# Counting the edges of an adjacency matrix by fours in a two-layer graph network

## The chip, the cores and the metric

The kernel runs on one core of a Trainium2 chip. The metric is the device time of one execution in microseconds. Inputs and outputs lie in the chip's main memory (DRAM), and the time covers the whole program from the first load to the last store. Engines are named as in the profile: PE does matrix products, PEld is its weight load, DVE, ACT and POOL are the vector, scalar and general engine, and SP issues transfers.

## What is computed

`x` is 4096 x 512 float32, `adj` is 4096 x 4096 int32 of zeros and ones with a density of 0.0078 (some 32 edges a row). Two layers follow each other, each with a residual and a layer norm:

```python
Ab = A > 0
keep = Ab & (jnp.cumsum(Ab.astype(jnp.int32), axis=1) <= 64)
cnt = keep.sum(axis=1, keepdims=True)
nb_mean = (keep.astype(X.dtype) @ X) / jnp.maximum(cnt, 1.0)
xj = leaky_relu(nb_mean @ W_nb.T + b_nb)
xi = leaky_relu(X @ W_line.T + b_line)
layer0 = xi + jnp.where(cnt > 0, xj, 0)
# layer 1, with h the normed result of layer 0 plus x:
Wh = h @ W + bW
e = leaky_relu((Wh @ a1 + b1)[:, None] + (Wh @ a2 + b2)[None, :], 0.2)
e = jnp.where(adj > 0, e, -9e15)
layer1 = softmax(e, axis=1) @ Wh
```

What matters here is `keep`: of each row of `adj` only the first 64 edges count in layer 0, while layer 1 uses every edge. So each edge needs a mark that says "kept", "edge but not kept" or "no edge".

## The kernel before

The rows are cut into 32 blocks of 128, one row to a partition, and a block of `adj` into two chunks of 2048 columns: 64 chunks, counted by `s`. Each chunk goes through a small pipeline:

1. `load_adj` (L156, queue of SP) loads 128 x 2048 int32, 1 MB.
2. `edge` (L163, ACT) makes ones and zeros in bf16 with a steep sigmoid (L167), and sums them along the row into `cnts`.
3. `scan` (L172, DVE) runs along the row: a value starts at 66 and each column takes `max(value, 2) - edge` (L179). After the k-th edge it is 66 - k, so 65 down to 2 for the 64 kept edges, and 1 for every later one. The last value is carried to the row's second chunk through `ends` (L183). Multiplied by the edge itself (L184) this is the code: 0 for no edge, 1 for an edge that is not kept, 2 and more for one that is. Every second block, `count` (L189) turns `ends` into the number of kept edges.
4. `pack` (L198, ACT) casts the code to one byte (L202), and POOL's queue stores it in `code_d` (L203).

Layer 0's neighbour sum reads the codes of a block back with a transposing transfer (L428, L460), and `make_kt` (L248, ACT, L254) turns them into the 0/1 weights of the matmuls at L521 with a sigmoid whose threshold, `steep[:, 1:2]`, lies between 1 and 2. Layer 1 reads the codes again (L616) and masks by whether they are zero (L635).

The order on every engine is the order in which the program issues, written out by hand (`manual_schedule`). There are three stages around the change. In the first (span 36 to 235 us) row block `i` is multiplied by both weights of layer 0 (`linear`, L342, matmuls at L345). DVE transposes the x blocks for it (`turn_x`, L293, L299) and does additions (L375, L383, L435), ACT evicts PSUM (L413) and bends lines (L379). `codes_until` (L207) puts 20 chunks evenly among these rows: per step one load, `edge(q + 1)`, `scan(q)`, `pack(q - 1)`. In the second (235 to 700 us) PE does `keep @ (X W)`: 32 rows of blocks in four steps of 16 matmuls (L521), the tiles `kt` made two steps ahead in one of three buffers. `codes_step` (L235) adds 25/16 chunks to each row until all 64 are done, some 660 us into the span; here `scan` is issued at once, while `edge` and `pack` wait in `late_q` and come out one or two at a time behind a `make_kt` (`codes_late`, L229). The third stage is layer 1 and has no chunks. The tiles `a`, `edge`, `left` and `code` have two buffers each; the x blocks turned for the matmuls have three, and the PSUM accumulators six.

The lines that set this order in the second stage:

```python
        make_kt(s + 2)
        if g == 2:
            bend0(i - 1)
        codes_late()
...
        codes_step(start + int((s + 1) * RATE / NS))
```

Of the kernel before, what the change touches and what calls it, by code (L numbers as in the profile page):

```python
# [11 lines left out]
BF16 = mybir.dt.bfloat16  # L12
U8 = mybir.dt.uint8
I32 = mybir.dt.int32
AF = mybir.ActivationFunctionType
ALU = mybir.AluOpType
# [4 lines left out]
P = 128  # L21
SQ = 32
NEIGHBORS = 64.0
# [3 lines left out]
FAR = 1e30  # L27

STEEP = 4000.0
# [3 lines left out]
def two_layer_adj_gnn(  # L33
# [16 lines left out]
    nc = tc.nc  # L50
    N, C = x.shape
    NB = N // P
    NC = C // P
    NT = NB // 2
    CH = 2048
    NCH = N // CH
# [17 lines left out]
    ps_acc = ctx.enter_context(tc.tile_pool(name="ps_acc", bufs=6, space=PSUM))  # L74

    few = const.tile([P, 5], F32, name="few")
    two, steep, far, neg_half = few[:, 0:1], few[:, 1:3], few[:, 3:4], few[:, 4:5]
    for k, value in enumerate((2.0, -0.5 * STEEP, -1.5 * STEEP, FAR, -0.5)):
        nc.vector.memset(few[:, k : k + 1], value)


# [4 lines left out]
    ends = const.tile([P, NB], F32, name="ends")  # L86
# [50 lines left out]
    with ExitStack() as l0:  # L137
        adj_p = l0.enter_context(tc.tile_pool(name="l0_adj", bufs=2))
# [13 lines left out]
        loaded = {}  # L152
        edge_of = {}
        seen_of = {}

        def load_adj(s):  # L156
            if s < NB * NCH:
# [2 lines left out]
                nc.sync.dma_start(a, adj_blk(b)[:, ts(h, CH)])  # L160
                loaded[s] = a

        def edge(s):  # L163
            if s < NB * NCH:
                b, h = divmod(s, NCH)
                edge_of[s] = adj_p.tile([P, CH], BF16, name="edge")
                nc.scalar.activation(  # L167
                    edge_of[s], loaded.pop(s), AF.Sigmoid, bias=steep[:, 0:1], scale=STEEP,
                    accum_out=cnts[:, h, b : b + 1],
                )  # L170

        def scan(s):  # L172
            if s < NB * NCH:
                b, h = divmod(s, NCH)

                left = adj_p.tile([P, CH], BF16, name="left")
                e = edge_of.pop(s)
                end = ends[:, b : b + 1]
                nc.vector.tensor_tensor_scan(  # L179
                    left, two.to_broadcast([P, CH]), e,  # L180
                    NEIGHBORS + 2.0 if h == 0 else end, ALU.max, ALU.subtract,
                )
                nc.vector.tensor_copy(end, left[:, CH - 1 : CH])  # L183
                nc.vector.tensor_tensor(left, e, left, ALU.mult)  # L184
                seen_of[s] = left
                if h == NCH - 1 and b % 2:
                    count(b - 1)

        def count(b):  # L189
            two_b = slice(b, b + 2)  # L190
            cnt = stat.tile([P, 2], F32, name="cnt")
            nc.vector.tensor_scalar(cnt, ends[:, two_b], 2.0, -1.0, ALU.max, ALU.mult)
            nc.vector.tensor_scalar_add(cnt, cnt, NEIGHBORS + 2.0)
            nc.vector.tensor_scalar(some[:, two_b], cnt, 0.0, None, ALU.is_gt)
            nc.vector.tensor_scalar_max(cnt, cnt, 1.0)
            nc.vector.reciprocal(rcnt[:, two_b], cnt)

        def pack(s):  # L198
            if 0 <= s < NB * NCH:
                b, h = divmod(s, NCH)  # L200
                code = adj_p.tile([P, CH // 2], BF16, name="code")
                nc.scalar.copy(code.bitcast(U8), seen_of.pop(s))  # L202
                nc.gpsimd.dma_start(code_d[b][:, ts(h, CH // 2)], code)  # L203

        done = [0]
# [1 line left out]
        def codes_until(s):  # L207

            while done[0] < min(s, NB * NCH + 1):
                q = done[0]  # L210
                if q == 0:
                    load_adj(0)
                    load_adj(1)
                    edge(0)
                load_adj(q + 2)
                edge(q + 1)
                scan(q)
                pack(q - 1)
                done[0] += 1
# [5 lines left out]
        def pack_late(q):  # L225
            pack(q)
            packed[0] = q + 1
# [7 lines left out]
        def codes_step(s):  # L235
            while done[0] < min(s, NB * NCH + 1):
                codes_late(2)
                q = done[0]
                load_adj(q + 2)
                scan(q)  # L240
                late_q.extend([(edge, q + 1), (pack_late, q - 1)])
                done[0] += 1
# [17 lines left out]
        with ExitStack() as la:  # L260
# [44 lines left out]
            def early(name):  # L305
                dt = I32 if name == "a" else BF16
                t = adj_p.tile([P, CH], dt, name=name).bitcast(F32)
                return t.rearrange("p (c q) -> p c q", q=C)

            raw = {}  # L310
            for name in ("nb", "line"):
                t = early("a")
                raw[name] = [t[:, c, :] for c in range(NC)]
            raw["w"] = []
            for k in range(2):
                t = early("left")
                raw["w"] += [t[:, c, :] for c in range(NC // 2)]
            early_rows = []
            for k in range(2):
                t = early("edge")  # L320
# [482 lines left out]
    cnt, idle = cnts[:, 0, :], cnts[:, 1, :]  # L803
# [17 lines left out]
    for s in range(NS):  # L821
# [13 lines left out]
        if FIRST <= s < FIRST + 8:  # L835
            b, i = divmod(s - FIRST, NI)
            mask(b, i)
            score(b, i)
        if FIRST + 4 <= s < FIRST + 12:
            b, i = divmod(s - FIRST - 4, NI)  # L840
# [4 lines left out]
        if s in range(FIRST + 14, FIRST + 22, 2):  # L845
            q, part = divmod((s - FIRST - 14) // 2, 2)
# [5 lines left out]
    for q in range(NP * NT):  # L852
        g, k = divmod(q, NP)
# [5 lines left out]
        b = {2: 2 * g + 3, 3: 2 * g + 4}.get(k, 2 if q == 0 else NB)  # L859
# [29 lines left out]
    p, rz = banks[NT - 1], rzs[NT - 1]  # L889
# [59 lines left out]
```

## Time and profile before

| | us |
|---|---|
| median of 3 runs | 1599.97 (1599.85 to 1600.56) |
| the profiled execution | 1600.12 |
| its span, first instruction to last | 1598.4 |
| PE busy in it | 1579.6 |
| DVE busy | 1305.4 |
| ACT busy | 924.2 |
| scans, L179, 64 of them | 284.5 |
| products, L184, 64 | 78.4 |
| edges, L167, 64 | 127.4 |
| packs, L202, 64 | 120.5 |

The busy row of the page gives, for each engine, the busy time in us, its share of the span and (x) the number of instructions. The chain of waits goes back from the last instruction, at each step to what released it, and gives each engine's share of the span. A wait reads "who waited, its line <- for whom: us in total, times, longest". A group or tile row gives the line, engine and operation, the count, the duration in ns (mean, or minimum/median/maximum) and the shape as partitions x elements with types, the output first. Busy matmuls are modelled and overlap, so the time from the start of one to the start of the next tells PE's pace better than the busy share. The granted clock of PE is 0.997 of full speed over the span.

### The profile page before, as it was taken

How to read it: one execution, taken by the hardware profiler on the slowest of the kernel's cores; microseconds unless marked ns; L12 is line 12 of the kernel's file. 1: busy time of each engine (PE TensorE's matmuls, PEld its weight loads, DVE VectorE, ACT ScalarE, POOL GpSimd, SP SyncE). 2: the span in 40 equal slices, each digit the busy share in tenths (PEclk: the TensorE clock that was granted, in tenths of full speed). 3: DMA queues.
4: the chain of work that ended last, by engine and by line, in shares of the span. 5: the costliest groups of instructions: out<-in, count | busy, mean ns of one | idle time of the engine just before them, and what ended most of it. 6: DMA issues, size and time to landing. Idle time of an engine off the chain costs nothing.

```text
span 1598.4 us, 18483 instructions
## 1 busy us (share of the span) xinstructions
PE 1579.6 (99%) x6456; PEld 1218.4 (76%) x6456; DVE 1305.4 (82%) x2154; ACT 924.2 (58%) x1086; POOL 260.0 (16%) x396
## 2 busy tenths in 40 slices
PE   8999999999999999999999999999999999999997
PEld 4444448888888888864378888888888888888886
DVE  4999986999999999555888887878888888788863
ACT  2655556777777777514237755557755557655520
POOL 4455531122223122210000000000000000000000
PEclk9999999999999999999999999999999999999999
DMA  8887867676757666444201111111111111211100
GB/s 195 287 259 236 265 217 224 215 220 211 229 189 228 206 215 191 116 103 122 76 27 28 53 54 41 52 36 34 53 47 47 48 28 44 54 41 53 40 7 33
DMA packets 168364, 192.73 MB, mean 121 GB/s; under 512 B 101408, under 2 KB 134464, under 8 KB 160080
## 3 DMA queue, kind: packets, MB, share of 16 engines
q1 hardware_dynamic: 147968, 131.38, 29.4%
q0 software_dynamic: 19728, 59.27, 11.0%
q8 instruction: 50, 0.82, 0.2%
q10 hardware_dynamic: 576, 0.92, 0.2%
q14 instruction: 42, 0.34, 0.1%
HBM read 132.65 MB, written 42.08 MB: 109 GB/s over the span
## 4 chain that ended last, share of the span: by engine, by line
PE 92%; DVE 3%; DMA 2%; issue 1%; ACT 1%; SPq 0%; POOL 0%; DVEq 0%; POOLq 0%; ACTq 0%
PE acc L739 34%; PE acc L521 29%; PE pt L739 14%; PE acc L345 9%; PE acc L825 5%; DMA c<-in_x_dram 1%; DVE left L179 1%; DMA a<-in_L_gnn_W_line_dram 1%; DMA edge<-in_L_gnn_a_dram 0%; DVE edge L361 0%; DVE xt L299 0%; DMA w<-x_d 0%; DVE y_lo L435 0%; DVE t L375 0%; ACT w L635 0%
## 5 line engine op out<-in xcount | busy, mean ns | idle before, releaser
L521 PE MATMUL acc<-y_hi,kt 128*128 128x512 f32 x1016 | 395.2, 389 | 0.0
L521 PE MATMUL acc<-y_lo,kt 128*128 128x512 f32 x1016 | 395.2, 389 | 0.0
L739 PE MATMUL acc<-bt,s 128*128 128x256 f32 x1536 | 342.6, 379 | 0.0
L739 PEld LDWEIGHTS acc<-bt,s 128*128 128x128 f32 x1536 | 291.8, 190 | 39.7
L635 ACT ACTIVATE w<-nat,few 128x1024 f32<-128x1024 uint8 x128 | 136.9, 1135 | 290.1 <-DVE a L699 238.8
L126 POOL TENSOR_TENSOR rs<-ve,few 128x1 f32<-128x1 f32 x64 | 76.2, 1191 | 969.3 <-DVE ve L124 969.2
L739 PE MATMUL acc<-bt,a 128*128 128x256 f32 x1024 | 232.1, 379 | 0.0
L739 PE MATMUL pt<-bt,a 128*128 128x256 f32 x1024 | 231.5, 379 | 0.0
L521 PEld LDWEIGHTS acc<-y_hi,kt 128*128 128x128 f32 x1016 | 190.8, 188 | 39.7
L521 PEld LDWEIGHTS acc<-y_lo,kt 128*128 128x128 f32 x1016 | 190.6, 188 | 39.5
L739 PEld LDWEIGHTS pt<-bt,a 128*128 128x128 f32 x1024 | 194.6, 190 | 26.9 <-issue 0.5
L254 ACT ACTIVATE kt<-ktb,few 128x1024 fp32r<-128x1024 uint8 x124 | 142.9, 1152 | 124.7 <-PE acc L521 107.8
L739 PEld LDWEIGHTS acc<-bt,a 128*128 128x128 f32 x1024 | 194.6, 190 | 26.5
L699 DVE STREAM_TRANSPOSE a<-w 128x1024 f32<-128x1024 f32 x128 | 153.0, 1224 | 57.8 <-ACT w L680 53.2
L627 ACT ACTIVATE w<-w,st_n 128x1024 f32<-128x1024 f32 x128 | 149.4, 1233 | 39.5 <-DVE m L638 39.5
L638 DVE CUSTOM_DVE_ANT_0 w<-e_n,w 128x1024 f32<-128x1024 f32 x128 | 149.6, 1221 | 9.6 <-ACT w L635 8.2
L167 ACT ACTIVATE edge<-a,few 128x2048 bf16<-128x2048 int32 x64 | 127.4, 1991 | 43.4 <-DVE left L184 20.3
L680 ACT ACTIVATE w<-w,nm 128x1024 f32<-128x1024 f32 x128 | 145.4, 1136 | 11.3 <-DVE nm L671 11.3
L179 DVE TENSOR_TENSOR_SCAN left<-few,edge 128x2048 bf16<-128x2048 f32 x32 | 141.3, 4415 | 12.7 <-ACT edge L167 10.9
L179 DVE TENSOR_TENSOR_SCAN left<-few,ends,edge 128x2048 bf16<-128x2048 f32 x32 | 143.2, 4475 | 2.3 <-ACT code L202 2.3
L202 ACT CAST code<-left 128x2048 uint8<-128x2048 bf16 x64 | 120.5, 1882 | 0.0
L345 PE MATMUL acc<-wt_nb,xt 128*128 128x512 f32 x256 | 115.5, 594 | 2.8 <-DVE xt L299 2.0
(135 smaller groups left out, 1521.3 us busy)
## 6 DMA issues: line engine op xcount, KB each, us to landing
a<-in_adj_dram SPq DMA_DIRECT2D x64, 1024.0 KB, 5.3
code_d<-code POOLq DMA_DIRECT2D x64, 256.0 KB, 3.7
nat<-code_d SPq DMA_DIRECT2D x256, 64.0 KB, 2.0
own_d<-xb POOLq DMA_DIRECT2D x32, 256.0 KB, 5.9
w<-x_d SPq DMA_DIRECT2D x128, 64.0 KB, 2.0
c<-in_x_dram POOLq DMA_DIRECT2D x124, 64.0 KB, 5.6
xb<-in_x_dram POOLq DMA_DIRECT2D x31, 256.0 KB, 5.8
own<-own_d SPq DMA_DIRECT2D x31, 256.0 KB, 2.8
```

The source lines that it names most:

```text
L167: nc.scalar.activation(edge_of[s], loaded.pop(s), AF.Sigmoid, bias=steep[:, 0:1], scale=STEEP, accum_out=cnts[:, h, b : b + 1],)
L179: nc.vector.tensor_tensor_scan(left, two.to_broadcast([P, CH]), e, NEIGHBORS + 2.0 if h == 0 else end, ALU.max, ALU.subtract,)
L202: nc.scalar.copy(code.bitcast(U8), seen_of.pop(s))
L254: nc.scalar.activation(kts[s], bytes_.rearrange("p t (i r) -> p t r i", r=2), AF.Sigmoid, bias=steep[:, 1:2], scale=STEEP,)
L345: nc.tensor.matmul(pl, lhs_t[:, k, :], w_t[name][:, k, :], start=(k == 0), stop=(k == NC - 1),)
L521: nc.tensor.matmul(accs[i], kt[:, k // 2, k % 2, :], term[:, j, :], start=(j == 0 and term is y_hi), stop=(j == NB - 1 and term is y_lo),)
L627: nc.scalar.activation(dst, src, AF.Prelu, bias=bias, scale=scale, alpha=0.2)
L635: nc.scalar.activation(w_i, nats[b, i // 2].bitcast(U8)[:, i % 2, :], AF.Relu, bias=far, scale=-FAR)
L638: nc.vector.tensor_tensor_reduce(w_i, e2_n, w_i, 1.0, -3e38, ALU.subtract, ALU.max, m4s[b][:, i : i + 1])
L680: nc.scalar.activation(w_i, w_i, AF.Exp, bias=nms[b][:, i : i + 1], accum_out=z4s[g][:, r, i : i + 1])
L699: nc.vector.transpose(a[:, r].rearrange("p s (i a) -> p i s a", a=SQ), wts[2 * g + r][:, :, ts(k, 8 * SQ)].rearrange("p i (s x) -> p i s x ...
L739: nc.tensor.matmul(banks[g][n], lhs[:, j, :], bt[:, 4 * k + j, rhs, :], start=(k == 0 and j == 0 and n == mate[0]), stop=(k == NP - 1 and ...
```

## The change

A chunk's columns are seen in groups of four neighbours. ACT's edge activation now reads the int32 columns so that `edge` holds four runs of 512: all first members of the groups, then all second, third and fourth ones. DVE adds first and second as well as third and fourth members (one instruction on 2 x 512), then the two sums (512), and scans the sums of four: 512 steps instead of 2048. The value starts at 69, is held at 5 or more, and gives what is left behind each group's fourth column. What is left behind the third is that plus the fourth's edge, behind the second the value behind the fourth plus the sum of third and fourth, and so on: one addition on 512 and one on 2 x 512. The product with the edges is as before. A kept edge now has a code of 5 or more, one that isn't kept 1 to 4, so the threshold of the weights is 4.5, and `count` uses 5 and 69. The pack reads the four runs in turn, so that the stored codes stand in the order of the columns as before. `scan` is split into two functions that are called one after the other.

```diff
--- before.py
+++ after.py
@@ -74,8 +74,8 @@
     ps_acc = ctx.enter_context(tc.tile_pool(name="ps_acc", bufs=6, space=PSUM))
 
     few = const.tile([P, 5], F32, name="few")
-    two, steep, far, neg_half = few[:, 0:1], few[:, 1:3], few[:, 3:4], few[:, 4:5]
-    for k, value in enumerate((2.0, -0.5 * STEEP, -1.5 * STEEP, FAR, -0.5)):
+    five, steep, far, neg_half = few[:, 0:1], few[:, 1:3], few[:, 3:4], few[:, 4:5]
+    for k, value in enumerate((5.0, -0.5 * STEEP, -4.5 * STEEP, FAR, -0.5)):
         nc.vector.memset(few[:, k : k + 1], value)
 
 
@@ -160,37 +160,57 @@
                 nc.sync.dma_start(a, adj_blk(b)[:, ts(h, CH)])
                 loaded[s] = a
 
+        def fours(t):
+
+            return t.rearrange("p (q t) -> p q t", q=4)
+
         def edge(s):
             if s < NB * NCH:
                 b, h = divmod(s, NCH)
-                edge_of[s] = adj_p.tile([P, CH], BF16, name="edge")
+                edge_of[s] = fours(adj_p.tile([P, CH], BF16, name="edge"))
                 nc.scalar.activation(
-                    edge_of[s], loaded.pop(s), AF.Sigmoid, bias=steep[:, 0:1], scale=STEEP,
+                    edge_of[s], loaded.pop(s).rearrange("p (t q) -> p q t", q=4),
+                    AF.Sigmoid, bias=steep[:, 0:1], scale=STEEP,
                     accum_out=cnts[:, h, b : b + 1],
                 )
 
         def scan(s):
+            scan_sums(s)
+            scan_codes(s)
+
+        def scan_sums(s):
             if s < NB * NCH:
                 b, h = divmod(s, NCH)
 
-                left = adj_p.tile([P, CH], BF16, name="left")
-                e = edge_of.pop(s)
+
+                left = fours(adj_p.tile([P, CH], BF16, name="left"))
+                e = edge_of[s]
                 end = ends[:, b : b + 1]
+                nc.vector.tensor_tensor(left[:, 0:2], e[:, 0:4:2], e[:, 1:4:2], ALU.add)
+                nc.vector.tensor_tensor(left[:, 2], left[:, 0], left[:, 1], ALU.add)
                 nc.vector.tensor_tensor_scan(
-                    left, two.to_broadcast([P, CH]), e,
-                    NEIGHBORS + 2.0 if h == 0 else end, ALU.max, ALU.subtract,
+                    left[:, 3], five.to_broadcast([P, CH // 4]), left[:, 2],
+                    NEIGHBORS + 5.0 if h == 0 else end, ALU.max, ALU.subtract,
                 )
-                nc.vector.tensor_copy(end, left[:, CH - 1 : CH])
+                nc.vector.tensor_copy(end, left[:, 3, CH // 4 - 1 :])
+                seen_of[s] = left
+
+        def scan_codes(s):
+            if s < NB * NCH:
+                b, h = divmod(s, NCH)
+                left, e = seen_of[s], edge_of.pop(s)
+
+                nc.vector.tensor_tensor(left[:, 1], left[:, 3], left[:, 1], ALU.add)
+                nc.vector.tensor_tensor(left[:, 0:4:2], left[:, 1:4:2], e[:, 1:4:2], ALU.add)
                 nc.vector.tensor_tensor(left, e, left, ALU.mult)
-                seen_of[s] = left
                 if h == NCH - 1 and b % 2:
                     count(b - 1)
 
         def count(b):
             two_b = slice(b, b + 2)
             cnt = stat.tile([P, 2], F32, name="cnt")
-            nc.vector.tensor_scalar(cnt, ends[:, two_b], 2.0, -1.0, ALU.max, ALU.mult)
-            nc.vector.tensor_scalar_add(cnt, cnt, NEIGHBORS + 2.0)
+            nc.vector.tensor_scalar(cnt, ends[:, two_b], 5.0, -1.0, ALU.max, ALU.mult)
+            nc.vector.tensor_scalar_add(cnt, cnt, NEIGHBORS + 5.0)
             nc.vector.tensor_scalar(some[:, two_b], cnt, 0.0, None, ALU.is_gt)
             nc.vector.tensor_scalar_max(cnt, cnt, 1.0)
             nc.vector.reciprocal(rcnt[:, two_b], cnt)
@@ -199,7 +219,10 @@
             if 0 <= s < NB * NCH:
                 b, h = divmod(s, NCH)
                 code = adj_p.tile([P, CH // 2], BF16, name="code")
-                nc.scalar.copy(code.bitcast(U8), seen_of.pop(s))
+                nc.scalar.copy(
+                    code.bitcast(U8).rearrange("p (t q) -> p t q", q=4),
+                    seen_of.pop(s).rearrange("p q t -> p t q"),
+                )
                 nc.gpsimd.dma_start(code_d[b][:, ts(h, CH // 2)], code)
 
         done = [0]
```

## The prediction

> **What bounds the kernel now.** I read the page first, its busy row and its chain of waits, then the busy time by stretches, cut where PE's work changes (x is the number of instructions).
>
> ```profile
> PE 1579.6 (99%) x6456; PEld 1218.4 (76%) x6456; DVE 1305.4 (82%) x2154; ACT 924.2 (58%) x1086; POOL 260.0 (16%) x396
> PE 92%; DVE 3%; DMA 2%; issue 1%; ACT 1%; SPq 0%; POOL 0%; DVEq 0%; POOLq 0%; ACTq 0%
> ```
> ```profile
> core 0: us, PE busy (x) PEld busy (x) DVE busy (x) ACT busy (x) POOL busy (x), PEclk, DMA share, GB/s
> 36.00:90.00 54.00, 51.85 (x120) 22.36 (x119) 48.29 (x49) 30.66 (x34) 23.76 (x43) 1.00 0.85 275
> 90.00:235.00 145.00, 145.00 (x339) 64.22 (x338) 139.34 (x152) 78.68 (x88) 74.45 (x135) 1.00 0.80 250
> 235.00:660.00 425.00, 425.00 (x1875) 351.57 (x1874) 383.32 (x471) 316.70 (x278) 98.33 (x103) 1.00 0.67 206
> ```
>
> PE is the bound in all three stretches in which adjacency chunks are worked: 15 of the 64 chunks in 90 to 235 us, about 44 in 235 to 660 us (43 edges, 45 packs by the groups of that window), the other five in 36 to 90 us. A pipelined engine can look busy without being at its rate, so I checked the pace in the timeline: from 450 us on the L521 matmuls start 0.2267 us apart without one exception, 64 of them to a row of blocks, so 14.5 us a row. Nothing that DVE or ACT does better can shorten that. The waits say the same from the other side: ACT waits for PE, not PE for ACT.
>
> ```profile
> ACT kt L254 <- PE acc L521: 107.8, 91, 2.5
> PEld acc L345 <- DVE xt L299: 5.1, 5, 1.9
> PE acc L345 <- DVE xt L299: 2.0, 2, 1.1
> ```
>
> The third line is all that the scan costs PE today: two gaps (0.94 us before 48.4 us and 1.10 us before 56.6 us in PE's timeline) in which PE wants a transposed x block that DVE makes only after a scan. So the most that this change can give back is 2.0 us, 0.13% of the time. Everything else DVE saves is saved beside a busy PE. What matters is whether something new gets slower than PE; the candidate is ACT, whose cover is the idle time in the third stretch: 425.0 - 316.7 = 108.3 us.
>
> **DVE, per chunk.** The rows, from the tile and shape views:
>
> ```profile
> L183 DVE CAST ends<-left x64: 153/154/157, 45.7 to 651.2; 128x1 f32<-128x1 bf16 x64
> L184 DVE TENSOR_TENSOR left<-edge,left x64: 1224/1224/1228, 45.9 to 651.4; 128x2048 bf16<-128x2048 bf16 x64
> L179 DVE TENSOR_TENSOR_SCAN left<-few,edge x32: 4409/4415/4425, 41.2 to 638.3; 128x2048 bf16<-128x2048 f32 x32
> L179 DVE TENSOR_TENSOR_SCAN left<-few,ends,edge x32: 4469/4476/4484, 49.4 to 646.7; 128x2048 bf16<-128x2048 f32 x32
> ```
>
> Two f32 tensor_tensor shapes give the fixed part: 692 ns at 512 elements (L715) and 420 ns at 256 (L768) make 1.06 ns per element and 148 ns fixed. With 148 ns fixed, the bf16 L184 runs at (1224-148)/2048 = 0.525 ns and the scan at (4415-148)/2048 = 2.08 ns per element. Now: 4.445 (mean scan) + 0.154 + 1.224 = 5.82 us. After: two additions of 1024 at 0.686, two of 512 at 0.417, the scan of 512 at 1.245 (mean of the forms), the copy 0.154, the product 1.224: together 4.83 us. DVE gains 0.99 us per chunk, 64 us in all, of which PE can use 2. All operands of the additions are runs of 512 adjacent bf16, so I take L184's pace. From the other side: if the split views made the additions run at the f32 pace, they cost 1.24 and 0.69, and a chunk takes 6.48 us, 0.66 more than now; if the product did too, 1.76 more. The new constants and the counting (L192, L193) keep their instructions. No instruction is moved in the order of any queue; no DMA is added, and the loads on SP and the stores on POOL (L203) keep place and size.
>
> **ACT, per chunk.** The instructions stay two, but both get strided reads. The edge activation (L167, median 1.987 us, int32) reads every fourth element, 16 bytes apart; the pack (L202, 1.882 us) reads its four neighbours from four runs 1024 bytes apart, a hop at every element. The trace has no such read. Bounds by rows: below, no cost: L254 already reads uint8 at a step of two (1152 ns) against 1136 ns for the same operation from its other buffer, and L635's plain read of the same size takes 1135 ns. That step stays within a few bytes, so the row is near in form and far in distance. Above: the slowest stream in the trace is the scan, 4415/2048 = 2.16 ns per element, 4.42 us for 2048: +2.43 for the edge and +2.54 for the pack. Between: the paces that this trace shows on DVE lie a factor of two apart (0.525, 1.06, 2.08 ns), and I take one such step for a read that no longer brings neighbours together. ACT's slope is (1987-1152)/1024 = 0.815 ns (L167 against L254), so a step costs 2048 x 0.815 = 1.67 us per instruction, 3.34 us per chunk. This is an estimate, near the middle of the bounds.
>
> The third stretch then needs 316.7 + (43+45) x 1.67 = 463.7 us of ACT in 425 us: 38.7 us too much. ACT works ahead by two kt tiles (make_kt(s+2); 2 x 3.63 us of matmuls less the 1.15 us of a kt, and a wait of about 0.5): 5.6 us of lag are free. PE therefore ends this stretch 33 us later. Behind the slower edge and pack in ACT's queue stand the kt activations (L254) that PE waits for; that is the new wait, PE for kt. In 90 to 235 us ACT goes to 78.7 + 15 x 3.34 = 128.8 of 145 us, which still fits; there PSUM evictions (L413) queue behind 7.2 us of edge and pack, which three rows of accumulators, 20 us of matmuls, cover. The first two PE gaps: the first scan waits for its edge (DVE's 10.9 us idle on L167), which comes 1.67 us later and gives 0.99 back; I book the gaps at zero.
>
> [...]
>
> Sum: the profiled execution took 1600.12 us (span 1598.4 and 1.7 around it), 0.15 above the median of 1599.97, so one base serves. 1600 + 33 = **1633 us**.
>
> **Rivals.**
> 1. *The strided reads are hidden (not slower).* One mechanism: ACT's idle time in the third stretch. It decides at (108.3 + 5.6)/44 = 2.59 us added per chunk; below, PE never waits for a kt. For it: L254's step of two costs at most 17 ns against L635's plain read, and if only one of the two instructions pays a step, 1.67 is below the bound. Time: 1600; with both free also the two gaps go, 1598. Against: both reads leave the neighbourhood that L254's step keeps.
> 2. *Both pay more, up to the scan's pace.* 43 x 2.43 + 45 x 2.54 = 219 us in the third stretch, less 108.3 and 5.6: +105. In 90 to 235 us 78.7 + 15 x 4.97 = 153.3, +8; before it five chunks add 25 to an idle of 23.3, +2. Time 1715. [...]
> 3. *The additions run at the f32 pace, the reads are free.* DVE in 90 to 235 us: 139.3 + 15 x 0.66 = 149.2 of 145, +4; in the third stretch 383.3 + 29 = 412 of 425, hidden. Time 1605; with the product at 1.76 more, 1600 + 21 + 36 + 6 = 1663. Against it: operands in runs like L184's.
> 4. *The change does not do what it says*: the short scan keeps a long fixed time. With 1 us more per scan DVE is where it was, and the time is decided by ACT as above.
>
> **How the numbers follow.** The forecast (both reads about one step of two) 0.46; rival 2, clearly more than that, 0.20; rival 1 0.28; rival 3 with 4's ill case 0.06. The measurement can tell about 0.2% from no change, 3.2 us. Since only 2.0 us can be won, faster by that much gets 0.02, for something on PE's path that I overlook; same 0.26, slower 0.72. The cases of no change and of a loss lie far apart, so the range goes from 1598 (rival 1) to 1720 (rival 2 and a little); the likeliest case's own range is 1608 to 1660, 2.8 to 4.0 us added per chunk with ACT's surplus landing on PE.
>
> **What would show it.** Right: scan rows of about 1.2 us, additions of 0.69 and 0.42; edge and pack rows near 3.7 and 3.6 us; in the third stretch ACT near 99% busy, DVE lower, PE with gaps, the wait "ACT kt for PE" gone and "PE for ACT kt" in its place, and the third stretch longer by some 33 us while 830 us and after are only shifted. Wrong: edge and pack at their old durations (then 1598 to 1600 and the 48 and 56 us gaps gone), or one of them alone doubled (then no change). If both rows are doubled and the time still stands, my step from ACT's surplus to PE's wait is what failed.

## The result and the profile after

The changed kernel takes **1660.27 us** (median of four, 1658.5 to 1661.05) against 1600.18 us before: a ratio of 1.0374 with a 95% interval of 1.0356 to 1.0392. The forecast was slower at 1633 us, with a range of 1598 to 1720. The profiled execution took 1661.05 us with a span of 1659.3 us, 60.9 us longer than the span before.

The busy row of the page, to be held against the same row of before:

```profile
PE 1595.0 (96%) x6456; PEld 1214.2 (73%) x6456; DVE 1241.2 (75%) x2410; ACT 1165.0 (70%) x1086; POOL 220.8 (13%) x396
```

DVE gave up 64.2 us, as worked out. ACT took on 240.8 us with the same number of instructions. PE has gaps: its work is the same, and 60.9 - (1595.0 - 1579.6) = 45.5 us of new idle time lie in its span. The other 15.4 us are counted as busy: the last matmul ahead of a pause shows its whole 0.39 us, where the next one otherwise starts after 0.23, the first behind a pause is shown with 0.50 us, and eight in the first stage took 1.7 us more (see the end). The tile rows of the two ACT instructions and of the scan say which durations moved (minimum/median/maximum in ns):

```profile
L171 ACT ACTIVATE edge<-a,few x64: 3915/3992/4118, 41.1 to 705.1; 128x2048 bf16<-128x2048 int32 x64
L222 ACT CAST code<-left x64: 3766/3875/3955, 55.3 to 722.5; 128x2048 uint8<-128x2048 bf16 x64
L191 DVE TENSOR_TENSOR_SCAN left<-few,left x32: 1223/1224/1226, 46.4 to 707.2; 128x512 bf16<-128x512 f32 x32
```

The edge went from 1.987 to 3.992 us and the pack from 1.882 to 3.875 us, both with the same element counts as before; only the order of their reads changed. Busy time by stretches, with two parts from inside the third stretch below it:

```profile
core 0: us, PE busy (x) PEld busy (x) DVE busy (x) ACT busy (x) POOL busy (x), PEclk, DMA share, GB/s
90.00:235.00 145.00, 145.00 (x339) 64.22 (x338) 126.31 (x212) 136.60 (x88) 76.66 (x140) 1.00 0.77 250
235.00:660.00 425.00, 386.50 (x1638) 303.50 (x1637) 291.38 (x551) 416.31 (x244) 51.38 (x89) 1.00 0.62 186
250.00:400.00 150.00, 137.63 (x590) 109.14 (x589) 98.97 (x187) 150.00 (x86) 16.79 (x29) 1.00 0.61 188
400.00:560.00 160.00, 144.14 (x612) 112.88 (x611) 114.65 (x220) 160.00 (x95) 20.41 (x34) 1.00 0.62 185
```

In the third stretch ACT was busy for 316.7 us before and is for 416.3 now, 98% of it; from 250 to 560 us it has no pause, while PE has: the bound has changed engine. In 90 to 235 us PE still is without a gap, with ACT at 94%. The waits name the place, the same two partners as before with the roles turned:

```profile
PEld acc L544 <- ACT kt L277: 65.6, 53, 2.1
PE acc L544 <- ACT kt L277: 43.7, 51, 1.6
ACT kt L277 <- PE acc L544: 15.4, 7, 2.5
```

ACT's own order shows why a `kt` comes late: between the activations that PE needs there now lie 4 us of work on an edge or a code.

```profile
454.74 2.19 ACT L277 ACTIVATE kt<-ktb,few 128x1024 fp32r<-128x1024 uint8 x2
456.83 3.96 ACT L171 ACTIVATE edge<-a,few 128x2048 bf16<-128x2048 int32 x1
460.70 0.18 ACT L171 ACTIVATION_READ_ACCUMULATOR edge<-a,few 128x1 f32 x1
460.79 1.14 ACT L277 ACTIVATE kt<-ktb,few 128x1024 fp32r<-128x1024 uint8 x1
461.83 3.91 ACT L222 CAST code<-left 128x2048 uint8<-128x2048 bf16 x1
```

Each instruction begins where the one before it ends, or up to 0.1 us earlier. The L544 matmuls start at 238.2 us (235.2 before), and the matmuls of layer 1 come 62.6 us later than before, so 59.6 us arise while the chunks of the second stage are worked and 3.0 us ahead of it; 1.7 us of this are gone again at the end of the span.

### The profile page after: what moved, and what is told of

The parts are those of the page before. It is cut to its first block, busy times and chain, and to the rows that moved or that the text cites. A ratio compares the mean times of both kernels' runs of the same rounds, so it can differ in the third digit from the quotient of the medians.

```text
span 1659.3 us, 18739 instructions
## 1 busy us (share of the span) xinstructions
PE 1595.0 (96%) x6456; PEld 1214.2 (73%) x6456; DVE 1241.2 (75%) x2410; ACT 1165.0 (70%) x1086; POOL 220.8 (13%) x396
## 4 chain that ended last, share of the span: by engine, by line
PE 55%; DVE 1%; ACT 1%; DMA 0%; issue 0%; SPq 0%; POOLq 0%; DVEq 0%; ACTq 0%
PE acc L762 33%; PE pt L762 13%; PE acc L848 5%; PE acc L544 4%; DMA w<-x_d 0%; ACT code L222 0%; DVE c L612 0%; ACT lm L650 0%; SPq L598 0%; ACT w L658 0%; ACT kt L277 0%; DVE bt L621 0%; DVE w L661 0%; ACT w L703 0%; DVE mm L683 0%
## 5 line engine op out<-in xcount | busy, mean ns | idle before, releaser
L544 PE MATMUL acc<-y_hi,kt 128*128 128x512 f32 x1016 | 401.7, 395 | 43.7 <-ACT kt L277 43.7
L544 PE MATMUL acc<-y_lo,kt 128*128 128x512 f32 x1016 | 396.3, 390 | 0.0
L544 PEld LDWEIGHTS acc<-y_hi,kt 128*128 128x128 f32 x1016 | 190.6, 188 | 104.7 <-ACT kt L277 65.6
L171 ACT ACTIVATE edge<-a,few 128x2048 bf16<-128x2048 int32 x64 | 255.9, 3998 | 10.1 <-DMA a<-in_adj_dram 9.6
L222 ACT CAST code<-left 128x2048 uint8<-128x2048 bf16 x64 | 247.3, 3864 | 0.0
L544 PEld LDWEIGHTS acc<-y_lo,kt 128*128 128x128 f32 x1016 | 190.8, 188 | 38.5
L722 DVE STREAM_TRANSPOSE a<-w 128x1024 f32<-128x1024 f32 x128 | 153.0, 1224 | 57.8 <-ACT w L703 53.2
L126 POOL TENSOR_TENSOR rs<-ve,few 128x1 f32<-128x1 f32 x64 | 38.8, 606 | 923.9 <-DVE ve L124 923.7
L277 ACT ACTIVATE kt<-ktb,few 128x1024 fp32r<-128x1024 uint8 x124 | 139.4, 1140 | 21.7 <-PE acc L544 15.4
L368 PE MATMUL acc<-wt_line,xt 128*128 128x512 f32 x256 | 115.2, 593 | 0.7 <-ACT wt_line L150 0.7
L848 PE MATMUL acc<-w,c 128*128 128x512 f32 x232 | 100.3, 593 | 2.6 <-DVE c L612 2.6
```

The costliest lines, as they stand in the source:

```text
L171: nc.scalar.activation(edge_of[s], loaded.pop(s).rearrange("p (t q) -> p q t", q=4), AF.Sigmoid, bias=steep[:, 0:1], scale=STEEP, accum_ou ...
L222: nc.scalar.copy(code.bitcast(U8).rearrange("p (t q) -> p t q", q=4), seen_of.pop(s).rearrange("p q t -> p t q"),)
L277: nc.scalar.activation(kts[s], bytes_.rearrange("p t (i r) -> p t r i", r=2), AF.Sigmoid, bias=steep[:, 1:2], scale=STEEP,)
L368: nc.tensor.matmul(pl, lhs_t[:, k, :], w_t[name][:, k, :], start=(k == 0), stop=(k == NC - 1),)
L544: nc.tensor.matmul(accs[i], kt[:, k // 2, k % 2, :], term[:, j, :], start=(j == 0 and term is y_hi), stop=(j == NB - 1 and term is y_lo),)
L722: nc.vector.transpose(a[:, r].rearrange("p s (i a) -> p i s a", a=SQ), wts[2 * g + r][:, :, ts(k, 8 * SQ)].rearrange("p i (s x) -> p i s x ...
```

## The experiments

Theory A is that the loss is ACT's time alone: added time is free up to the idle time that ACT had (the cover), 2.6 us per chunk, and goes to PE in full beyond it. The rivals are DVE's longer row of dependent instructions (B), strided reads that hold up memory for others (C), and a cost that is added without a cover. "Turn" is short for reordering a chunk: the edge turns columns into runs, the pack turns runs back into columns.

**One of the two reads plain.** The first kernel reads and writes the pack straight through:

```diff
-                    code.bitcast(U8).rearrange("p (t q) -> p t q", q=4),
-                    seen_of.pop(s).rearrange("p q t -> p t q"),
+                    fours(code.bitcast(U8)),
+                    seen_of.pop(s),
```

> The changed kernel with a pack that reads and writes the four runs straight through, so the codes are stored in the order of the runs and not of the columns (the weights of both layers then sit at wrong columns; the amount of work is the same). Theory A (the loss is ACT's time, 2.0 us each for edge and pack against a cover of about 2.6 us per chunk): pack back at 1.88 us, edge stays at 4.0, 2.0 us added is under the cover, 1597 to 1603 us. Rival B (the loss comes from DVE: six instructions that depend on each other where there were three): 1650 to 1660. If cost were simply added per slow instruction, without a cover: 1630.

The second does it for the edge:

```diff
-                    edge_of[s], loaded.pop(s).rearrange("p (t q) -> p q t", q=4),
+                    edge_of[s], fours(loaded.pop(s)),
```

> The changed kernel with an edge activation that reads straight through; the four members of a group are then columns 512 apart, and the pack still interleaves, so stored codes sit at wrong columns. Theory A: edge back at 1.99 us, pack stays at 3.87, 2.0 us added is under the cover, 1597 to 1602 us. Rival B (DVE): 1650 to 1660. Simply added: 1630.

Measured: 1598.42 us (ratio 0.9991, 0.9982 to 1.0000) and 1598.88 us (0.9992, 0.9982 to 1.0001). The third stretch of each, first with the plain pack, then with the plain edge:

```profile
235.00:660.00 425.00, 425.00 (x1877) 351.98 (x1876) 338.33 (x647) 393.38 (x279) 60.35 (x103) 1.00 0.69 205
```
```profile
235.00:660.00 425.00, 425.00 (x1877) 351.89 (x1876) 337.75 (x647) 401.87 (x278) 59.79 (x102) 1.00 0.70 205
```

ACT rises from 316.7 to 393 and 402 us of 425, and PE has no gap. Each read costs its 2 us and each alone is hidden: half of the added ACT time costs nothing, not half of the 60 us. A cost added without a cover would have given 1630.

**Both plain: the DVE part alone.** The two edits together.

> The changed kernel with edge and pack both straight through: the DVE part of the change alone. Groups are columns 512 apart, so which edges count as the first 64 of a row would differ in a row with more than 64 edges. Theory A: ACT as before, DVE 1 us less per chunk, the first two PE gaps gone: 1597 to 1600 us. Rival B (DVE's chain of dependent instructions is what delays): 1650 to 1660.

Measured: 1597.12 us (0.9984, 0.9974 to 0.9993). The DVE instructions are those of the changed kernel, and the time is 0.16% below before. Rival B falls. That 64 us of DVE work saved bring 2.7 us is what the profile of before allowed: in the stretches with chunks PE waited for DVE only in two early gaps.

**ACT's time added with plain reads.** In the kernel before, each edge and each pack are issued twice:

```diff
+                nc.scalar.activation(
+                    edge_of[s], loaded[s], AF.Sigmoid, bias=steep[:, 0:1], scale=STEEP,
+                )
...
+                nc.scalar.copy(code.bitcast(U8), seen_of[s])
```

> The kernel before, plain reads and the long scan, with each edge activation (first time without its sum) and each pack issued twice: ACT gets 1.9 + 1.8 = 3.7 us more per chunk with no strided read anywhere. Theory A: (3.7 - 2.6) x 44 = 48 us, 1635 to 1660 us. Rival C (the strided reads hurt by holding up memory for others, not by ACT's time): no more than 1605.

Measured: 1661.68 us (1.0382, 1.0366 to 1.0397), with the wait of the changed kernel:

```profile
PE acc L525 <- ACT kt L258: 43.0, 51, 1.7
```

Edge and pack read straight through here, and the loss is that of the change. Rival C falls. The time came out 2 us above the end of the range expected: I had counted the repeats as overlapping their predecessors, but in ACT's timeline they do not:

```profile
450.83 1.88 ACT L205 CAST code<-left 128x2048 uint8<-128x2048 bf16 x1
452.75 1.90 ACT L206 CAST code<-left 128x2048 uint8<-128x2048 bf16 x1
456.65 1.99 ACT L167 ACTIVATE edge<-a,few 128x2048 bf16<-128x2048 int32 x1
458.67 2.00 ACT L170 ACTIVATE edge<-a,few 128x2048 bf16<-128x2048 int32 x1
```

The second pack starts 1.92 us after the first and the second edge 2.02 us, together 3.94 us per chunk and not 3.7, nearly the change's 4.0.

**The ACT part alone, with the old scan.**

```diff
-                    edge_of[s], loaded.pop(s), AF.Sigmoid, bias=steep[:, 0:1], scale=STEEP,
+                    edge_of[s].rearrange("p (q t) -> p q t", q=4),
+                    loaded.pop(s).rearrange("p (t q) -> p q t", q=4),
+                    AF.Sigmoid, bias=steep[:, 0:1], scale=STEEP,
...
-                nc.scalar.copy(code.bitcast(U8), seen_of.pop(s))
+                nc.scalar.copy(
+                    code.bitcast(U8).rearrange("p (t q) -> p t q", q=4),
+                    seen_of.pop(s).rearrange("p (q t) -> p t q", q=4),
+                )
```

> The kernel before with its scan of 2048 columns, but edge and pack read as in the changed kernel: the ACT part of the change alone. The scan then counts in the order of the four runs, so which edges are the first 64 would differ in a row with more. Theory A: ACT is the bound whatever DVE does, 1655 to 1668 us, a little above the changed kernel since DVE's first chunks are slower. Rival: the strided reads only hurt together with DVE's reads of the runs: 1600 to 1605.

Measured: 1662.17 us (1.0387, 1.0369 to 1.0404), edge 3.971 and pack 3.868 us (means). With ACT as the bound, the long or the short scan makes 2 us of difference, and the two intervals overlap.

**The turn on the write side.** The same reordering, with the jumps meant to be in the writes:

```diff
-                    edge_of[s], loaded.pop(s).rearrange("p (t q) -> p q t", q=4),
+                    edge_of[s].rearrange("p q t -> p t q"),
+                    loaded.pop(s).rearrange("p (t q) -> p q t", q=4),
...
-                    code.bitcast(U8).rearrange("p (t q) -> p t q", q=4),
-                    seen_of.pop(s).rearrange("p q t -> p t q"),
+                    code.bitcast(U8).rearrange("p (t q) -> p q t", q=4),
+                    seen_of.pop(s),
```

> The changed kernel with the turn moved from the reads to the writes: the edge activation reads the columns straight through and writes each to its run (2-byte writes that hop 1024 bytes), and the pack reads the runs straight through and writes every fourth byte. Every value and place as in the changed kernel. If only reads that hop cost (the stream has to wait for what it fetches, a write need not be waited for): both rows near 2.0 and 1.9 us, 1596 to 1599 us. If a hop costs the same on either side: 4.0 and 3.9 us, 1660. If only the hop of 1024 bytes costs and a step of four bytes does not: edge 4.0, pack 1.9, one of two, 1597 to 1603.

Measured: 1906.51 us (1.1917, 1.1899 to 1.1935), outside all three ranges. That a write need not be waited for, the reason given with the first guess, no run shows. The third had only the order right, a costly edge and a nearly free pack:

```profile
L171 ACT ACTIVATE edge<-a,few 128x2048 bf16<-128x2048 int32 x64 | 612.5, 9578 | 5.4 <-DMA a<-in_adj_dram 5.4
L223 ACT CAST code<-left 128x2048 uint8<-128x2048 bf16 x64 | 165.8, 2590 | 0.0
```

The edge's output now goes through the runs in turn, so every element is written 1024 bytes or more away from the one before it. Its input keeps the view by fours in this text, and no view of the profile shows in which order the words are read. Either way the writes are what is costly: the strided read with straight writes takes 3.99 us in the changed kernel, this instruction 9.6 us, and straight reads with such writes take 9.4 us by themselves (below). The pack's writes at a step of four bytes cost only 0.7 us more than plain ones. PE's granted clock was 0.946 over this run, so its time is not a measure of ACT's part alone.

**The steps by themselves.** A kernel of its own that times ACT copies of 2048 elements, for instance

```python
read("r_word_16B", wide.rearrange("p (t q) -> p q t", q=4))
read("r_half_hop", half.rearrange("p (q t) -> p t q", q=4))
```

> No layer is computed, zeros are stored: one load, then ACT copies of 2048 elements by themselves, three times each, which differ only in the step of the read (4, 8, 16, 32, 64 bytes of 4-byte words, pairs of words; 2, 4, 8, 16 bytes of 2-byte halves, hops of 1024 bytes, pairs that hop) or of the write (the same for halves; 1 to 16 bytes of bytes). The plain ones should take 1.8 to 1.9 us, the 16-byte words and the hopping halves 3.7 to 3.9 as in the changed kernel (if they take 1.9 here, the cost is contention in the kernel and not the pattern). If the bound is two elements within 16 bytes, words at 8 bytes, halves at 8 bytes and pairs are plain and halves at 16 bytes are not; if the cost grows with the step, 32 and 64 bytes take more than 16.

One execution; some of the groups (busy us, mean ns of one), in the page's order of cost:

```profile
L78 ACT COPY w_half_hop<-halves 128x2048 bf16<-128x2048 bf16 x3 | 28.1, 9376 | 0.0
L78 ACT COPY w_half_16B<-halves 128x2048 bf16<-128x2048 bf16 x3 | 27.9, 9297 | 0.0
L92 ACT CAST w_byte_8B<-halves 128x2048 uint8<-128x2048 bf16 x3 | 14.8, 4919 | 0.0
L55 ACT CAST r_word_32B<-words 128x2048 bf16<-128x2048 int32 x3 | 11.5, 3847 | 0.0
L55 ACT CAST r_word_16B<-words 128x2048 bf16<-128x2048 int32 x3 | 11.3, 3777 | 0.0
L55 ACT COPY r_half_16B<-halves 128x2048 bf16<-128x2048 bf16 x3 | 11.3, 3777 | 0.0
L55 ACT COPY r_half_hop<-halves 128x2048 bf16<-128x2048 bf16 x3 | 10.9, 3625 | 0.0
L92 ACT CAST w_byte_4B<-halves 128x2048 uint8<-128x2048 bf16 x3 | 7.4, 2457 | 0.0
L90 ACT CAST w_byte_1B<-halves 128x2048 uint8<-128x2048 bf16 x3 | 6.6, 2194 | 0.0
L55 ACT COPY r_half_8B<-halves 128x2048 bf16<-128x2048 bf16 x3 | 6.0, 1983 | 0.0
L55 ACT CAST r_word_8B<-words 128x2048 bf16<-128x2048 int32 x3 | 5.9, 1983 | 0.0
L55 ACT COPY r_half_hop_pair<-halves 128x2048 bf16<-128x2048 bf16 x3 | 5.8, 1944 | 0.0
L55 ACT CAST r_word_4B<-words 128x2048 bf16<-128x2048 int32 x3 | 5.7, 1893 | 0.0
L92 ACT CAST w_byte_2B<-halves 128x2048 uint8<-128x2048 bf16 x3 | 5.7, 1890 | 0.0
```

Alone the two reads take 3.78 and 3.63 us, in the kernel 3.99 and 3.88; so at least nine tenths of each duration come with the pattern and not from contention, and where the last 0.2 us come from stays open. Reads show two prices here: 1.9 to 2.0 us at steps of up to 8 bytes (words at 8 bytes, halves at 8 bytes) and for pairs that hop, and 3.6 to 3.85 us otherwise, whether the step is 16, 32, 64 or 1024 bytes; no step between 8 and 16 bytes was run. Writes go up in stairs: 1.89 at 2 bytes, 2.46 at 4, 4.9 at 8 and 9.3 to 9.4 at 16 bytes or a hop. One row does not fit: bytes written without a step took 2.19 us here, more than at 2 bytes, while the plain pack in the kernel takes 1.88.

**The cover, measured from below.** The changed kernel with the pack's turn alone on the write side (the second half of the diff of the write-side kernel).

> The changed kernel with one edit: the pack reads the four runs straight through and writes every fourth byte, which took 2.46 us against 1.89 alone and 2.59 in the kernel with both turns on the write side. Every value and place as in the changed kernel. Added to ACT per chunk: 2.0 for the edge and 0.7 for the pack, 2.7 us. Theory A with the cover measured by the two kernels that lie above it (57 us over 44 chunks is 1.3 us beyond it, of 3.94 to 4.0 added: cover 2.65): within a few us of the edge, 1597 to 1605 us. If the cover were no threshold and time simply grew with ACT's added time, 60/4.0 x 2.7: 1640.

Measured: 1600.26 us (1.0000, 0.9991 to 1.0009). The third stretch:

```profile
235.00:660.00 425.00, 425.00 (x1873) 351.35 (x1872) 336.98 (x643) 415.29 (x278) 59.50 (x102) 1.00 0.69 204
```

The two instructions, mean of all 64 in ns behind the busy time:

```profile
L171 ACT ACTIVATE edge<-a,few 128x2048 bf16<-128x2048 int32 x64 | 257.2, 4019 | 9.7 <-DMA a<-in_adj_dram 6.0
L222 ACT CAST code<-left 128x2048 uint8<-128x2048 bf16 x64 | 161.7, 2526 | 0.0
```

ACT stands at 98% and PE still has no gap: 2.03 + 0.64 = 2.67 us added per chunk are just covered, while 3.94 us (the doubled instructions) and 3.99 us (the change) cost 62 and 60 us. Time against ACT's added time is flat and then steep.

**By twos, with no slow step.** The steps point to a version in which no ACT instruction pays: two runs of 1024, words read at 8 bytes, bytes written at 2.

```diff
-            return t.rearrange("p (q t) -> p q t", q=4)
+            return t.rearrange("p (q t) -> p q t", q=2)
...
-                    edge_of[s], loaded.pop(s).rearrange("p (t q) -> p q t", q=4),
+                    edge_of[s], loaded.pop(s).rearrange("p (t q) -> p q t", q=2),
...
-                nc.vector.tensor_tensor(left[:, 0:2], e[:, 0:4:2], e[:, 1:4:2], ALU.add)
-                nc.vector.tensor_tensor(left[:, 2], left[:, 0], left[:, 1], ALU.add)
+                nc.vector.tensor_tensor(left[:, 0], e[:, 0], e[:, 1], ALU.add)
...
-                nc.vector.tensor_tensor(left[:, 1], left[:, 3], left[:, 1], ALU.add)
-                nc.vector.tensor_tensor(left[:, 0:4:2], left[:, 1:4:2], e[:, 1:4:2], ALU.add)
+                nc.vector.tensor_tensor(left[:, 0], left[:, 1], e[:, 1], ALU.add)
...
-                    code.bitcast(U8).rearrange("p (t q) -> p t q", q=4),
-                    seen_of.pop(s).rearrange("p q t -> p t q"),
+                    code.bitcast(U8).rearrange("p (t q) -> p q t", q=2),
+                    seen_of.pop(s),
```

The scan holds at 3 and starts at 67, and the threshold of the weights is 2.5.

> Counting by twos: the edge reads words at a step of 8 bytes into two runs of 1024 (1.98 alone), the scan has 1024 steps and holds at 3, one addition makes the sums and one what is left behind the first of each pair, and the pack reads the runs straight through and writes every second byte (1.89 alone). Every value of the result as before. ACT gets 0.1 us more per chunk, DVE goes from 5.8 to 0.69 + 2.28 + 0.15 + 0.69 + 1.22 = 5.0 us. Theory A: nothing but the early PE gaps can change, 1596 to 1599 us, as in the kernel with both reads plain. If step-8 reads or 2-byte writes cost more inside the kernel than alone: up to 1605.

Measured: 1596.86 us (0.9984, 0.9975 to 0.9992), below both kernels, by 0.16% against before. Edge 2.138 us, pack 1.894 us (means), scans 2.29 and 2.35 us; the busy time of two stretches:

```profile
36.00:90.00 54.00, 54.00 (x127) 23.93 (x126) 46.55 (x63) 32.78 (x35) 25.70 (x47) 1.00 0.89 288
235.00:660.00 425.00, 425.00 (x1877) 352.22 (x1876) 346.93 (x558) 322.70 (x279) 66.35 (x103) 1.00 0.69 206
```

PE is without a gap in 36 to 90 us too (51.85 of 54 before), so from there to 660 us a faster scan has nothing left to give.

## Why the prediction was right, and where its size was off

- *PE is the bound, a faster scan can give 2.0 us.* Right: by their medians the DVE part alone gave 2.7 us and the version by twos 3.2; the ratio of both is 0.9984, 2.6 us, with about 1.4 us to either side.
- *DVE per chunk 5.82 to 4.83 us.* Right to 1%: scans of 1224 and 1284 ns (1215 and 1275 worked out), additions of 687 and 692 (686), 425 and 416 (417). The split views of runs kept the pace of L184, so rival 3 did not happen.
- *The strided reads fall on ACT, and PE waits for `kt`.* Right, place and direction; shown from both sides, by taking the reads away one at a time and by adding ACT time without them.
- *1.67 us per instruction, "one step of a factor of two" on ACT's slope.* This is the term that was too small: measured 2.00 for the edge and 1.99 for the pack. The factor was borrowed from the paces of three DVE rows, since no ACT row had such a read; that it came out near two is luck as far as its reason goes. The slope more than doubled, from 0.815 to 0.815 + 2.0/2.048 = 1.79 ns per element. My bounds, 0 and 2.43 (2.54), held it. With the measured sizes the prediction's own sum gives 43 x 2.00 + 45 x 1.99 - 108.3 - 5.6 = 61.7 us in the third stretch, against 59.6 measured. Since only what goes beyond the cover counts, a term 20% larger made the loss 82% larger (60.1 us, not 33). The time, 1660.27, lies just past the end of the likeliest case's own range, 1608 to 1660.
- *The cover, 2.59 us per chunk from idle time and two tiles of lead.* Right: the kernel with 2.67 us added still shows no gap, and 59.6 us from 44 chunks with 3.99 added put it at 3.99 - 59.6/44 = 2.64.
- *The two early gaps booked at zero.* Off by 3 us in the profiled execution. The second went, but the first grew from 0.94 to 3.66 us, and the eight matmuls behind it were 1.7 us slower than usual:

```profile
51.35 5.40 PE L368 MATMUL acc<-wt_nb,xt 128*128 128x512 f32 x8 [3.66 <-DVE xt L322]
```

  The first edge started at 41.1 us, 2.0 us later than before, after its load, and took 2.0 us more, of which the short scan gave one back. The kernels with the pack plain and with the pack's turn on the write side have the same edge and scan; there the first edge started at 38.7 and 39.4 us (DVE waited 12.2 and 12.9 us for it, 14.5 here), and the gaps were none and one of 0.43 us. So most of the 3 us goes with the late load, which no other profile here shows; why it came later was not tried.

## What to carry to other kernels

Before shortening the work of an engine that nobody waits for, look at which engine pays for the new layout: here 1 us saved on DVE per chunk was bought with 4 us on ACT. The time added to an engine off the path cost nothing here up to its idle time in that stage, and what went beyond it cost in full (2.67 us per chunk none, 3.94 us 62 us in all); so compute the idle time per item first, and be most careful about the size of a term when it lands near that edge. When ACT must reorder elements, read at steps of up to 8 bytes or let pairs of neighbours hop (1.9 to 2.0 us for 2048 elements here, against 3.6 to 3.85 at 16 bytes and more), or write at steps of 2 bytes (1.89 us), or of 4 (2.46 us) if there is room: for 2048 elements the patterns measured here cost about 0, 0.6, 2, 3 or 7.5 us more than plain ones.

## What was not expected of the hardware

- **Reads on ACT had two prices, writes a staircase** (the groups above). Words read at a step of 8 bytes took 1.98 us and at 16 bytes 3.78, and wider steps about the same (3.85 us at 32 bytes, 3.61 at 64). Writes of halves went on rising, 2.46 us at 4 bytes, 4.92 at 8 and 9.30 at 16, and those that hop took 9376/1888 = 5 times as long as the plain ones (w_half_2B).
- **An instruction of POOL lasted as long as the scan beside it.** In the timeline of the kernel before:

```profile
406.23 4.47 DVE L179 TENSOR_TENSOR_SCAN left<-few,ends,edge 128x2048 bf16<-128x2048 f32 x1
406.46 4.60 POOL L126 TENSOR_TENSOR rs<-ve,few 128x1 f32<-128x1 f32 x1 [3.57 <-DVE ve L124]
```

  This power of one column otherwise took 0.56 us. Its mean fell from 1191 to 606 ns in the changed kernel and was 692 ns by twos, where the long ones last 2.6 us beside scans of 2.3 us. PE waited for none of them.
- **Behind a pause of 3.66 us PE was slow for a while.** The eight matmuls behind it took 5.40 us where 3.70 is usual, and the granted clock of that stretch (36 to 90 us) was 0.97; behind the 3.40 us pause of the kernel with ACT's instructions doubled eight took 3.70 at 1.00. The many pauses of up to 1.6 us in the third stretch left it at 1.00, while the kernel with hopping writes, whose PE was busy 114 of 145 us in 90 to 235 us, ran at 0.93 there. So the slow spell came behind the one pause of 3.66 us and not behind that of 3.40, and no run was made to find what sets it.
